# Attention scores kept in one PSUM bank per head: row maxima subtracted once per query block, later key tiles added as key differences

## The chip, the cores and the metric

One core of a Trainium2 chip runs the whole program. The metric is the device time of one execution in microseconds; the kernel before takes 2413.94 us (median of 3 runs, 2413.16 to 2414.01). Engines: TensorE (PE, its weight loads listed apart as PEld), VectorE (DVE), ScalarE (ACT), GpSimd (POOL) and SyncE (SP, which here only issues DMAs). Each engine works through its own queue strictly in the order in which the program was compiled.

## The reference

A transformer block with conditioning, on x of shape (2, 2048, 512) in float32:

```python
mod = silu(condition) @ Wada + bada            # shift, scale, gate, twice
xm = layernorm(x) * (1 + sc_a) + sh_a
q, k, v = split(xm @ Wqkv)                     # 16 heads of 32
scores = einsum('bhqd,bhkd->bhqk', q, k) * 32 ** -0.5
scores = where(causal, scores, -inf)
out = softmax(scores) @ v
x = x + gt_a * (out @ Wproj + bproj)
xm = layernorm(x) * (1 + sc_m) + sh_m
x = x + gt_m * (gelu(xm @ W1 + b1) @ W2 + b2)
```

What matters here is the softmax: the kernel computes exp(score - row maximum), so that every score tile needs the row maximum subtracted before the exponential.

## The kernel before

The two batch rows are done one after the other: QKV stage, attention phase, projection; then one MLP for both (W1 and W2 in a seven-product form whose weight sums are made on POOL ahead of time).

**QKV stage** (class `Qkv`, line 753). Tokens come in NG = 4 groups of 512. `group` (line 795) makes, for each of the C = 4 chunks f of 128 columns (four heads), q and then k as a transposed product of four accumulating matmuls (`ps_qk`, in a PSUM pool of 6 banks), and last four tiles of v. Of each q and k, ACT writes the high part (fp32r) and DVE the rest into a tile `hl` (a pool of 4 buffers), and SP stores it in DRAM (`qd`, `kd`). After chunk 0 of a group SP loads the keys and queries of that chunk back, with high and low parts stacked on the partitions: 4 heads x 32 become a contraction of 128 rows (kh, kl, kh, kl against qh, qh, ql, ql). Between the matmuls of groups 1 to 3 `among` puts **score banks** (`Row.score`, `bank`, lines 484 and 435): a 128-query by up to 512-key product on PE (tile `s`, 2 banks) whose maximum over the keys is taken by DVE. These only serve the row maxima.

**Quarters** (line 880) prepares the MLP weights: each `step` has POOL issue four DMAs of W1 or W2, wait for them, add and subtract five pairs, and issue the store. Sixteen steps are spread over the QKV stages, six in that of batch row 0 (group 3) and ten in that of row 1. Only instructions marked with `act` or `mm` keep the order in which they are written; the rest is put in order by the compiler's scheduler, so a quarter step may stand earlier in POOL's queue than its line suggests.

**Attention phase** (line 529). A unit is a pair (c, i) of a chunk of four heads and a block of 512 queries; there are 16 a row, in the order i = 0, 1, 2, 3 for c = 0 and 0, 2, 1, 3 after that. A unit has 4i + 3 steps, one key tile of 128 each (`steps_of`, line 646): 4i full tiles, then the diagonal ones: the whole-width tile, a step with the 384- and 128-wide tiles side by side, and the 256-wide one. `scores_t` (line 538) makes one step for the four heads:

- a matmul with `sel` (minus ones) and `fold[u % 2]` (rows of maxima, made by `rows` from one unit's maxima) starts a fresh bank `st` with the negative maximum of each query; four of them, one per head, each of 32 contraction rows;
- a matmul of the keys and queries adds the scores to that bank;
- ACT takes the exponential into a tile `e` (E_BUFS = 16, four steps' worth); on diagonal steps POOL masks it (`affine_select`, line 585);
- score banks of later units (up to AHEAD = 3 ahead) stand between these, as many as `due` and `count` ask for; within a step the third one borrows a bank of `st`.

Two steps later (LAG = 2) `flush` issues `values`, the product with v into `o`. Row sums go through POOL: `begin_chain` and `add_to` (lines 613 and 609) add the `e` of four steps and a product with ones (`sm`) follows; the last unit of a row adds on DVE. `finish` copies `o` and `sm` out.

Keys of the next chunk go to one of two tiles `kst0`, `kst1` in one load of 4 MB (line 672), used both by the score banks and by `scores_t`.

Of the kernel before, what the change touches and what calls it, by code (L numbers as in the profile page):

```python
# [8 lines left out]
F32 = mybir.dt.float32  # L9
# [18 lines left out]
def dit_block_kernel(  # L28
# [55 lines left out]
    def pool(name, bufs=1, **kw):  # L84
# [21 lines left out]
    tmask = bp.tile([P, TQ + 1], F32, tag="tmask", name="tmask")  # L106
    nc.vector.tensor_reduce(
        tmask[:, :TQ],
# [4 lines left out]
    nc.vector.tensor_copy(tmask[:, TQ:], tmask[:, TQ - 1 : TQ])  # L113
    fold, mhl = [], []
    for n in range(2):

        f = bp.tile([P, QB + P], F32R, tag=f"fold{n}", name=f"fold{n}")
        fold.append(f)
# [9 lines left out]
    def picks():  # L128
# [35 lines left out]
        [dram.tile([2, P, T], F32, tag=f"k{b}{c}", name=f"k{b}{c}") for c in range(C)]  # L164
        for b in range(B)
# [116 lines left out]
    class Row:  # L282


        def __init__(self, b):
            self.b = b
            self.vv = bp.tile([P, NT, D], F32, tag="vv", name="vv")
            self.kst, self.qst, self.pools = {}, {}, {0: bp}
# [12 lines left out]
        def load_keys(self, c, g, n=1):  # L301

            tok = slice(g * MT, (g + n) * MT)
            if g == 0:
                self.kst[c] = self.pools[c % 2].tile(
                    [P, HC, T], F32R, tag=f"kst{c % 2}", name="kst"
                )
            for r in range(4):
                nc.sync.dma_start(
                    self.kst[c][r * HD : (r + 1) * HD, :, tok].bitcast(F32),  # L310
                    kd[self.b][c][r % 2, :, tok].rearrange("(h d) t -> d h t", d=HD),
                )
# [122 lines left out]
        def bank(self, u, h, t, kb, s):  # L435
# [6 lines left out]
                self.kst[c][:, h, kb * QB : kb * QB + w],  # L442
# [41 lines left out]
        def score(self, n, borrow=None):  # L484

            for k in range(n):
                if borrow and k % 2 == 0:  # L490
                    s = borrow()
                else:
                    s = ps_sp.tile([P, QB], F32, tag="s", name="s")
                item = self.todo.pop(0)
                u = item[0]
                if self.mx is None:
                    self.mx = bp.tile(
                        [P, HC * TQ, units[u][1] + 1], F32, tag="mx", name="mx", bufs=3
                    )
                self.bank(*item, s)  # L500
                if not self.todo or self.todo[0][0] != u:
                    self.split(u, self.mx, s)
                    self.mx = None
                    self.at += 1

        def rows(self, u):
# [8 lines left out]
                fold[u % 2].rearrange("p (t q) -> p t q", t=TQ + 1),  # L515
                ps.unsqueeze(1).to_broadcast([P, TQ + 1, P]),
                tmask.unsqueeze(2).to_broadcast([P, TQ + 1, P]),
# [11 lines left out]
    def attention_phase(row):  # L529
        b, vv, kst, qst = row.b, row.vv, row.kst, row.qst  # L530
        with pool(f"att{b}") as ap, pool(
            f"ps_st{b}", bufs=HC, space=PSUM
        ) as ps_stp, pool(f"ps_o{b}", space=PSUM) as ps_op:
            row.pools[1] = ap

            n_bank = [0]

            def scores_t(u, step, n):
# [6 lines left out]

                def st_bank():

                    n_bank[0] += u == len(units) - 1  # L550
                    if n_bank[0] % 6 >= HC:
                        return ps_sp.tile([P, QB], F32, tag="s", name="st")
                    return ps_stp.tile([P, QB], F32, tag="st", name="st")

                c, i = units[u]
                tiles = steps_of[u][step]
                q0 = tiles[0][1]
                w = sum(QB - q for _, q in tiles)
                sts, es = [], []
                for h in range(HC):  # L560
                    g = slice(h * HD, (h + 1) * HD)
                    st = st_bank()
                    mm(
                        st[:, :w], sel[g, :], fold[u % 2][g, q0 : q0 + w],
                        start=True, stop=False,
                    )
                    sts.append(st)
                for h in range(HC):
                    at = 0
                    for j, q in tiles:  # L570
                        mm(
                            sts[h][:, at : at + QB - q],
                            kst[c][:, h, j * P : (j + 1) * P],
                            qst[u][:, h, q:],
                            start=False, stop=at + QB - q == w,
                        )
                        at += QB - q
                    e = ap.tile([P, QB], F32, tag="e", name="e", bufs=E_BUFS)
                    act(nc.scalar.activation(e[:, :w], sts[h][:, :w], AF.Exp))  # L579
                    if tiles[0][0] >= i * TQ:  # L580

                        d = e.rearrange("p (t k) -> p t k", k=P)[:, 0 : TQ : TQ - 1, :]
                        d = d[:, : len(tiles), :]
                        act(
                            nc.gpsimd.affine_select(  # L585
                                d, d, pattern=[[0, len(tiles)], [1, P]],
                                compare_op=ALU.is_ge, fill=0.0,
                                base=0, channel_multiplier=-1,
                            )
                        )  # L590
                    es.append(e)
                    if h < 2 and n >= 3 or h >= HC - n and n < 3:
                        row.score(1)
                if n >= 3:
                    row.score(1, st_bank)
                    row.score(min(n, HC) - 3)
                return es, max(0, n - HC)
# [42 lines left out]
            def flush(upto):  # L640
# [7 lines left out]
                + [[(i * TQ + 1, P), (i * TQ + 3, 3 * P)], [(i * TQ + 2, 2 * P)]]  # L648
# [882 lines left out]
```

## Time and profile before

| what | value |
|---|---|
| time, median of 3 runs | 2413.94 us |
| profiled execution, first to last instruction (span) | 2411.0 us |
| granted TensorE clock | 1.000 |
| st<-fold,sel matmuls | 1152, 148.6 us busy |
| POOL additions ee (row sums) | 592, 740.4 us busy |

The profiled execution has no separate timing; its span is 2.9 us below the median of the runs. Busy time of each engine by stage, in us, from the windows view:

| stage | from-to | us | PE | DVE | ACT | POOL | DMA share |
|---|---|---|---|---|---|---|---|
| QKV row 0, groups 0 (rest) to 3 | 40.0-212.8 | 172.8 | 172.8 | 91.8 | 31.9 | 41.4 | 0.66 |
| attention row 0 | 212.8-755.4 | 542.6 | 538.4 | 364.3 | 304.7 | 435.1 | 0.31 |
| projection row 0 | 755.4-812.1 | 56.7 | 56.7 | 38.0 | 4.3 | 32.1 | 0.76 |
| QKV row 1 | 812.1-1002.1 | 190.0 | 189.7 | 101.0 | 36.1 | 64.0 | 0.70 |
| attention row 1 | 1002.1-1543.7 | 541.6 | 537.7 | 364.1 | 304.6 | 435.0 | 0.31 |
| projection row 1, MLP | 1543.7-2411.0 | 867.3 | 856.5 | 368.3 | 204.4 | 111.4 | 0.34 |

A matmul's busy time runs from its start to its end, and the next one starts inside it, so PE is shown busy nearly everywhere; how dense it is must be read from the starts in the timeline. A line of the groups gives source line, engine, operation, output and input tiles, shapes, count, then busy time and mean duration, then idle time before and what ended it.

### The profile page before, as it was taken

The page shows a single profiled execution, that of the slowest core. Times are in us where ns is not written, and L with a number is a line of the kernel's source. Part 1 is how long each engine was busy: PE and PEld are TensorE (multiplying, and loading weights), DVE is VectorE, ACT ScalarE, POOL GpSimd, SP SyncE. Part 2 cuts the span into 40 slices and gives each one's busy share as a digit, 9 for nine tenths or more (in the row PEclk, how much of TensorE's full clock was granted, in tenths as well). Part 3 has the DMA queues.
Part 4 walks back from the last instruction along what each step waited for, and adds up shares of the span by engine and source line. Part 5 has one row for each costly group of instructions (what it writes and reads, how often), then busy time and mean ns, then how long its engine had stood idle before and what let it go on. Part 6 is the DMA issues. An engine that isn't in the chain of part 4 may idle for free.

```text
span 2411.0 us, 31023 instructions
## 1 busy us (share of the span) xinstructions
PE 2381.4 (99%) x10797; PEld 1167.1 (48%) x10797; DVE 1345.9 (56%) x2813; ACT 896.4 (37%) x1671; POOL 1125.3 (47%) x1279
## 2 busy tenths in 40 slices
PE   8999999999999999999999999999999999999998
PEld 4455555555544445555555554444444444444443
DVE  3466666766647446766676665663344263343424
ACT  2113555555563121355555555423213212312310
POOL 1062888978775560199897878432001101100200
PEclk9999999999999999999999999999999999999999
DMA  7677124051325794621505132552324233222323
GB/s 253 197 239 198 41 47 96 23 118 42 111 96 186 240 319 162 154 55 34 111 23 115 45 101 91 168 178 77 110 78 146 76 106 136 82 92 87 122 87 101
DMA packets 132854, 285.72 MB, mean 119 GB/s; under 512 B 13472, under 2 KB 42700, under 8 KB 127832
## 3 DMA queue, kind: packets, MB, share of 16 engines
q1 hardware_dynamic: 125936, 256.94, 36.1%
q0 software_dynamic: 6384, 26.25, 3.1%
q8 instruction: 85, 1.39, 0.2%
q14 instruction: 73, 0.60, 0.1%
q10 hardware_dynamic: 376, 0.55, 0.1%
HBM read 209.76 MB, written 81.79 MB: 121 GB/s over the span
## 4 chain that ended last, share of the span: by engine, by line
PE 96%; DVE 2%; POOL 1%; issue 0%; DMA 0%; ACT 0%; SPq 0%; DVEq 0%; POOLq 0%; ACTq 0%
PE st L199 19%; PE ps_h L199 16%; PE ps_y L199 16%; PE o L199 11%; PE s L199 10%; PE ps_qk L199 9%; PE ps_o L199 5%; PE ps_v L199 4%; PE sm L199 4%; PE ps_xt L207 1%; POOL ee L607 1%; PE ps_o L207 1%; DMA x<-in_x_dram 0%; DVE junk L449 0%; DVE mx L454 0%
## 5 line engine op out<-in xcount | busy, mean ns | idle before, releaser
L579 ACT ACTIVATE e<-st 128x512 f32<-128x512 f32 (+1 forms) x1152 | 574.7, 578 | 427.1 <-PE st L199 359.7
L607 POOL TENSOR_TENSOR ee<-ee,e 128x512 f32<-128x512 f32 x424 | 529.8, 1294 | 4.3 <-ACT e L579 4.0
L454 DVE TENSOR_REDUCE mx<-s 128x1 f32<-128x512 f32 x604 | 407.6, 687 | 203.6 <-PE s L199 202.5
L199 PE MATMUL s<-kst,qst 128*128 128x512 f32 (+3 forms) x1032 | 463.8, 451 | 4.7 <-DVE mx L454 2.9
L199 PE MATMUL st<-qst,kst 128*128 128x512 f32 (+3 forms) x1280 | 409.2, 387 | 0.0
L1295 POOL TENSOR_TENSOR c<-c 128x512 f32<-128x512 f32 x32 | 40.7, 1272 | 623.2 <-DVE c L1257 596.6
L199 PE MATMUL o<-e,vv 128*32 128x512 f32 (+3 forms) x2560 | 300.6, 538 | 2.0 <-POOL e L585 2.0
L199 PE MATMUL ps_h<-sx,w 128*128 128x512 f32 x640 | 286.7, 592 | 0.0
L449 DVE CUSTOM_DVE_ANT_0 junk<-s,causal 128x512 bf16<-128x512 f32 (+3 forms) x428 | 209.0, 488 | 132.9 <-PE s L199 125.2
L199 PE MATMUL ps_y<-sh,w 128*128 128x512 f32 x640 | 277.6, 592 | 0.0
L199 PEld LDWEIGHTS st<-qst,kst 128*128 128x128 f32 x1280 | 227.4, 188 | 94.2 <-issue 62.1
L199 PEld LDWEIGHTS s<-kst,qst 128*128 128x128 f32 x1032 | 194.4, 189 | 154.4 <-DVE mx L454 55.2
L607 POOL TENSOR_TENSOR ee<-e 128x512 f32<-128x512 f32 x168 | 210.6, 1288 | 100.8 <-ACT e L579 100.3
L199 PE MATMUL ps_qk<-xmT,wqkv 128*128 128x512 f32 x512 | 239.0, 594 | 1.8 <-DVE xmT L256 1.8
L1257 DVE TENSOR_TENSOR h<-c,ps_h 128x512 f32<-128x512 f32 x128 | 88.1, 688 | 232.4 <-PE ps_h L199 232.4
L585 POOL TENSOR_SCALAR_AFFINE_SELECT e<-e 128x128 f32<-128x128 f32 (+1 forms) x384 | 123.0, 364 | 195.7 <-ACT e L579 193.0
L199 PEld LDWEIGHTS ps_h<-sx,w 128*128 128x128 f32 x640 | 121.1, 190 | 150.2 <-issue 149.7
L199 PEld LDWEIGHTS ps_y<-sh,w 128*128 128x128 f32 x640 | 120.3, 190 | 144.9 <-issue 143.5
L1281 ACT ACTIVATE h<-h,cols 128x512 f32<-128x512 f32 x128 | 92.4, 722 | 182.0 <-DVE h L1257 182.0
L199 PE MATMUL st<-fold,sel 32*128 32x512 f32 (+1 forms) x1152 | 148.6, 481 | 0.6 <-ACT vv L836 0.2
L199 PEld LDWEIGHTS ps_qk<-xmT,wqkv 128*128 128x128 f32 x512 | 93.9, 190 | 96.9 <-issue 90.4
L199 PEld LDWEIGHTS st<-fold,sel 32*128 32x128 f32 x1152 | 59.1, 181 | 144.2 <-ACT e L579 86.6
(129 smaller groups left out, 2359.9 us busy)
## 6 DMA issues: line engine op xcount, KB each, us to landing
qst<-q SPq DMA_DIRECT2D x128, 256.0 KB
w<-w1d SPq DMA_DIRECT2D x34, 896.0 KB
w<-w2d SPq DMA_DIRECT2D x28, 1024.0 KB
kst<-k SPq DMA_DIRECT2D x24, 1024.0 KB
q<-hl SPq DMA_DIRECT2D x32, 512.0 KB
k<-hl SPq DMA_DIRECT2D x32, 512.0 KB
kst<-k SPq DMA_DIRECT2D x32, 256.0 KB
w<-in_L_cond_W_dram POOLq DMA_DIRECT2D x64, 128.0 KB, 5.6
```

Of the source, the lines that this page charges most:

```text
L199: return tc.keep_in_program_order(nc.tensor.matmul(*args, **kw))
L207: return tc.keep_in_program_order(nc.tensor.transpose(dst, src, ident[:n, :n]))
L449: nc.vector.tensor_tensor_reduce(junk[:, :w], s[:, :w], causal[:, QB - w :], 1.0, MASKED, ALU.add, ALU.max, m,)
L454: nc.vector.tensor_reduce(m, s[:, :w], axis=AX.X, op=ALU.max)
L579: act(nc.scalar.activation(e[:, :w], sts[h][:, :w], AF.Exp))
L585: nc.gpsimd.affine_select(d, d, pattern=[[0, len(tiles)], [1, P]], compare_op=ALU.is_ge, fill=0.0, base=0, channel_multiplier=-1,)
L607: act(engine.tensor_tensor(dst, x, y, ALU.add))
L1257: nc.vector.tensor_tensor(dst, x, y, op)
L1281: nc.scalar.activation(d, d, AF.Gelu, bias=col(r_b1 + chunk, 1))
L1295: nc.gpsimd.tensor_tensor(c1_, c1_, c2_, ALU.subtract)
```

## The change

A bank of scores now stays with its head for the whole unit. The first key tile adds the negative maxima and the scores as before; ACT reads the bank; the next tile adds the product of the queries with the **difference** of its keys and those of the tile before, in place, after the exponential has read the bank. So the `sel` matmul is issued once per head and unit instead of once per tile (unit 0 of each row keeps it, and the plain keys). The differences are made in the QKV stage by the new `gaps`, after each k: ACT copies the product into a tile `kf` whose first 128 columns POOL fills with the last tile of the previous group, DVE subtracts, ACT writes the high part, POOL the rest, and SP stores 512 KB in a new DRAM buffer `gd`.

With it: the pool of `hl` has 3 buffers, which q, k and the differences share; differences load into one tile `kgap` (16 DMAs of 256 KB per chunk, at the start of the phase and at three steps of a chunk's last unit and one of the next); the score banks keep a single tile of plain keys, reloaded head by head (`load_head`) after the last bank of each head; diagonal tiles pair up as (384), (256, 128), one after the other in the same bank, with `flush` between; score banks no longer borrow `st`; the last unit of a row no longer uses six banks.

```diff
-        f = bp.tile([P, QB + P], F32R, tag=f"fold{n}", name=f"fold{n}")
+        f = bp.tile([P, QB], F32R, tag=f"fold{n}", name=f"fold{n}")
...
+        def load_head(self, c, h):
+            for r in range(4):
+                nc.sync.dma_start(
+                    self.kst[r * HD : (r + 1) * HD, h, :].bitcast(F32),
+                    kd[self.b][c][r % 2, h * HD : (h + 1) * HD, :],
+                )
+        def load_gaps(self, c, g):
+            tok = slice(g * MT, (g + 1) * MT)
+            for r in range(4):
+                nc.sync.dma_start(
+                    self.kgap[r * HD : (r + 1) * HD, :, tok].bitcast(F32),
+                    gd[self.b][c][r % 2, :, tok].rearrange("(h d) t -> d h t", d=HD),
                 )
...
+                if i == NQ - 1 and c + 1 < C and self.todo[0][:2] != (u, h):
+                    self.load_head(c + 1, h)
...
-                for h in range(HC):
-                    g = slice(h * HD, (h + 1) * HD)
-                    st = st_bank()
-                    mm(
-                        st[:, :w], sel[g, :], fold[u % 2][g, q0 : q0 + w],
-                        start=True, stop=False,
-                    )
-                    sts.append(st)
-                for h in range(HC):
-                    at = 0
-                    for j, q in tiles:
+                keys = row.kgap if u else kst
...
+                for k, (j, q) in enumerate(tiles):
+                    if k:
+                        values()
+                    if j == 0 or u == 0:
+                        for h in range(HC):
+                            g = slice(h * HD, (h + 1) * HD)
+                            mm(
+                                sts[h][:, q:], sel[g, :], fold[u % 2][g, q:],
+                                start=True, stop=False,
+                            )
+                    for h in range(HC):
                         mm(
-                            sts[h][:, at : at + QB - q],
-                            kst[c][:, h, j * P : (j + 1) * P],
+                            sts[h][:, q:],
+                            keys[:, h, j * P : (j + 1) * P],
                             qst[u][:, h, q:],
-                            start=False, stop=at + QB - q == w,
+                            start=False, stop=True,
+                            skip_group_check=u > 0 and j > 0,
                         )
...
-                if n >= 3:
-                    row.score(1, st_bank)
-                    row.score(min(n, HC) - 3)
-                return es, max(0, n - HC)
+                return es, max(0, n - 3)
...
-                + [[(i * TQ + 1, P), (i * TQ + 3, 3 * P)], [(i * TQ + 2, 2 * P)]]
+                + [[(i * TQ + 1, P)], [(i * TQ + 2, 2 * P), (i * TQ + 3, 3 * P)]]
...
+        def gaps(self, g, f, ps, hp, tok):
+            kf = hp.tile([P, P + MT], F32, tag="kf", name="kf", bufs=2)
+            tail = self.tails[:, f, :]
+            if g == 0:
+                nc.gpsimd.memset(kf[:, :P], 0.0)
+            else:
+                nc.gpsimd.tensor_copy(kf[:, :P], tail)
+            nc.scalar.copy(kf[:, P:], ps)
+            if g + 1 < NG:
+                nc.gpsimd.tensor_copy(tail, kf[:, MT:])
+            d = kf[:, :MT]
+            nc.vector.tensor_tensor(d, kf[:, P:], d, ALU.subtract)
+            dl = hp.tile([P, 2, MT], F32R, tag="hl", name="dl", bufs=3)
+            nc.scalar.copy(dl[:, 0, :], d)
+            nc.gpsimd.tensor_tensor(dl[:, 1, :], d, dl[:, 0, :].bitcast(F32), ALU.subtract)
+            nc.sync.dma_start(
+                gd[self.row.b][f][:, :, tok].rearrange("l p t -> p l t"), dl.bitcast(F32)
             )
...
-                    hl = hp.tile([P, 2, MT], F32R, tag="hl", name="hl", bufs=4)
+                    hl = hp.tile([P, 2, MT], F32R, tag="hl", name="hl", bufs=3)
...
+                    if which == 1:
+                        self.gaps(g, f, ps, hp, tok)
```

## Prediction

> **What bounds the kernel now.** I read the page's busy shares first, then the costliest groups, then stretches of the attention phase, and last the timeline where the change acts. The page and two of its groups:
>
> ```profile
> PE 2381.4 (99%) x10797; PEld 1167.1 (48%) x10797; DVE 1345.9 (56%) x2813; ACT 896.4 (37%) x1671; POOL 1125.3 (47%) x1279
> ...
> L607 POOL TENSOR_TENSOR ee<-ee,e 128x512 f32<-128x512 f32 x424 | 529.8, 1294 | 4.3 <-ACT e L579 4.0
> ...
> L199 PE MATMUL st<-fold,sel 32*128 32x512 f32 (+1 forms) x1152 | 148.6, 481 | 0.6 <-ACT vv L836 0.2
> ```
>
> PE looks like the only bound, and the matmuls that the change removes are its own. But the shares are averages. Here are four units of chunk 1 of row 0 (i = 0, 2, 1, 3) and then the last unit, each from its first row-sum addition to that of the next; columns: length, then PE, PEld, DVE, ACT, POOL:
>
> ```profile
> 355.20:368.20 13.00, 13.00 (x125) 6.75 (x124) 5.95 (x12) 6.64 (x15) 2.81 (x9) 1.00 1.03 212
> 368.20:408.30 40.10, 40.10 (x255) 21.12 (x254) 29.12 (x62) 23.27 (x47) 38.30 (x41) 1.00 0.45 101
> 408.30:435.50 27.20, 26.87 (x191) 14.29 (x190) 19.02 (x62) 15.02 (x31) 23.43 (x29) 1.00 0.21 51
> 435.50:492.60 57.10, 57.10 (x373) 29.84 (x372) 39.59 (x99) 31.41 (x63) 54.32 (x56) 1.00 0.11 26
> ...
> 710.40:755.40 45.00, 44.46 (x330) 19.04 (x329) 33.58 (x51) 29.72 (x60) 12.94 (x17) 1.00 0.26 94
> ```
>
> POOL is busy 54.32 us of the 57.10 of an i = 3 unit: it stands just behind PE. At the end of such a unit the timeline shows PE already waiting for it:
>
> ```profile
> 542.29 2.52 POOL L585 TENSOR_SCALAR_AFFINE_SELECT e<-e 128x256 f32<-128x256 f32 x8
> ...
> 543.80 0.19 PEld L199 LDWEIGHTS o<-e,vv 128*32 128x32 f32 x8 [0.37 <-POOL e L585]
> ...
> 546.89 1.28 POOL L607 TENSOR_TENSOR ee<-e 128x512 f32<-128x512 f32 x1 [2.08 <-ACT e L579]
> ```
>
> So the loop is closed: POOL's masks release PE's value products, those release the next unit's scores, their exponentials release POOL's next additions.
>
> **Attention: what PE is spared.** Four `sel` matmuls and the next product in the timeline:
>
> ```profile
> 442.94 0.50 PE L199 MATMUL st<-fold,sel 32*128 32x512 f32 x4
> 443.38 0.50 PE L199 MATMUL st<-qst,kst 128*128 128x512 f32 x1
> ```
>
> The four hold PE for 443.38 - 442.94 = 0.44 us, 0.11 each. After the change a row issues 4 for each of 15 units and 16 in unit 0, 76, both rows 152; 1000 go, 110 us at PE's price. An i = 3 unit loses 14 of its 15 groups of four, 14 x 0.44 = 6.2 us.
>
> Weighed against this: the Trainium skill, "TensorEngine Tiling (Array Packing)", section "Theoretical Speedup", gives matmuls of at most 32 rows up to four times the speed. By it the four would cost about one 128-row slot (0.23 us, 444.06 to 444.30 in the same stretch), and I would estimate 57 us instead of 110. The trace shows 0.44, so the row decides.
>
> **Attention: what POOL lets through.** POOL's additions stay: 40 in an i = 3 unit, 28 in i = 2, 16 in i = 1. Back to back they take 1.25 us (eight in 10.0). Behind them stand the masks of the first two diagonal steps, now four 128-wide ones each, at 1.05 us for four. So POOL's chain from the first addition to the mask that releases PE is 40 x 1.25 + 2.1 = 52.1 us, and 37.1 and 22.1. From there to the next addition the trace shows 546.89 - 543.7 = 3.2 us here and 2.1 at the least elsewhere; without `sel` (0.44) and with a 384-wide tile alone, I take 2.5. Units can then not be shorter than 54.6, 39.6 and 24.6. PE alone would allow 57.1 - 6.2 = 50.9, so POOL decides. Savings of a row:
>
> - i = 3: 57.1, 57.1, 57.6 to 54.6: 8.0
> - i = 2: 42.4, 40.1, 40.4, 40.1 to 39.6: 4.6
> - i = 1: 25.4, 27.2, 26.7, 25.3 to 24.6: 6.2
> - i = 0: no additions on POOL, PE's price, 2 x 0.44 in three units: 2.7
> - the last unit adds on DVE (33.6 busy of 45): not POOL-bound; PE's price is 6.2, but it goes from six banks to four; I take 4
>
> Together 25.5, for two rows **-51**. Bounds: -110 if POOL did not bind, and about -20 if each of 32 units gave 1 us back. That upper end is for what before does not show: a bank's product now waits for the exponential of the same bank (ACT, four in 2.06 us), and the (256, 128) step does so twice, with four more exponentials a unit; and score banks take two PSUM banks and borrow none, so that a third score waits for DVE (0.69). Value products (1.0 us) and POOL's pace cover these in the units with i > 0; I take nothing. Queued behind such a wait on PE is everything, on ACT and POOL only work that depends on it.
>
> **Transfers.** Keys come twice (plain and differences): 256.94 MB at 36.1% of 2411 us is 0.295 MB/us, so 4 MB are 13.6 us of all 16 DMA engines. The attention phase uses 0.31 of them, so the sum fits. Chunk 0's differences must land before unit 1, and unit 0 is 17.5 us long. `load_head` waits for the last score bank of a head, and the next chunk's first bank is a step or two later; I take 3 us for six chunk changes, bounds 0 and 12.
>
> **QKV: what is added.** For each of 32 k tiles: ACT two copies (0.60 each in the `hl` rows), DVE one subtraction (0.69), POOL one subtraction (1.28, as in ee) and two 128-wide copies, SP one store (0.36 to issue). None of the engines is full: of 172.8 us DVE is busy 91.8, ACT 31.9, POOL 41.4. By throughput this is hidden, +0. But POOL's queue is in order, and the quarter steps stand in it:
>
> ```profile
> 127.09 4.32 POOL L923 DMA_DIRECT2D w<-in_L_cond_W_dram  x6 [108.69 <-DMA kst<-k]
> 135.53 0.73 POOL L931 TENSOR_TENSOR w<-w 128x256 f32<-128x256 f32 x1 [4.12 <-DMA w<-in_L_cond_W_dram]
> ...
> 149.22 1.46 POOL L923 DMA_DIRECT2D w<-in_L_cond_W_dram  x2 [3.88 <-DMA w1d<-w]
> ```
>
> This is the first of three pairs of steps, which run from 127.09 to 185.23 and mostly wait for their DMAs. In the compiled order of the changed program the POOL subtraction of group 2, chunk 2 stands behind the third pair. Its store is therefore late, and `hl` has three buffers shared by q, k and differences, so the difference of chunk 3 gets its buffer only when that store has landed. SP holds at that store, with the q and k stores and x loads behind it. ACT waits for the buffer at its high copy; behind it on ACT stand the next `hl` copies and v; behind those on DVE `hl`'s low part and then score maxima; PE goes on through its six product banks (four v, q, k of the next group) until its third score finds both score banks taken. Before, that score is here (group 3):
>
> ```profile
> 172.60 0.79 PE L199 MATMUL s<-kst,qst 128*128 128x512 f32 x1
> ```
>
> Steps end at 185.2, plus 2 for a later start and 4 for the additions now among them: 191. Subtraction 1.3, store 4 to land (a store of keys and its reload take 5.5), two ACT copies, `hl` and a maximum on DVE 2.6: PE goes on at about 199, +26. An earlier hold of some 10 us behind the first pair is contained in this, since the steps set the time. In row 1 the subtraction of group 0, chunk 2 stands in the fourth pair, just ahead of this store:
>
> ```profile
> 880.84 0.55 POOL L911 DMA_DIRECT2D w2d<-w  x1
> ```
>
> 880.8 + 4 + 1.3 is 886.1; with 4 and 2.6 as above PE goes on at 892.7. Before, the same third score starts at 865.94: +27. For the two-bank running afterwards I add 2 to each: **+57**. Bounds: +35 (stores landing at once, steps 8 us earlier each) and +75 (stores land later, since the DMA share is 0.96 in the first half of row 1's stage, and its later pairs hold again).
>
> **Sum.** 2411.0 - 51 + 3 + 57 = 2420; the median stands 2.9 us above the span, so **2423**. About 0.2% (4.8 us) is what a measurement can tell from no change.
>
> **Rivals.**
> - *The waits in QKV are covered.* POOL has 131 us idle in that stage, so the steps might end before PE needs the banks. This one ends on the other side: 2414 - 51 + 3 = 2366 with nothing lost. It decides below a QKV loss of 48 us. Against it: the order in POOL's queue is fixed, and 58 us of steps cannot hide behind six banks (about 20 us of products).
> - *POOL does not bind.* The additions' 3.2 us gap closes and PE's price counts: 2414 - 110 + 3 + 57 = 2364. Against it: 54.32 of 57.10 busy and the wait at 543.80.
> - *The attention gain is eaten* by the in-place waits on exponentials and the two score banks, 1 us a unit: 2414 - 20 + 3 + 57 = 2454.
> - That `sel` would not go is excluded by the compiled order: 152 are left.
>
> **How the numbers follow.** Forecast .55 (own range 2405 to 2440), QKV covered .17 (2350 to 2390), POOL not binding .08, gain eaten .20 (2440 to 2465). The range 2370 to 2458 leaves out half of the second, nearly all of the third, and little of the last: .18. Faster by over 0.2% (under 2409): .17 + .08 + .07 of the forecast's own = .32. Within: .13. Slower: .35 + .20 = .55.
>
> **What the changed profile would show.** st<-fold,sel x152. Stages of QKV at about 201 and 219 us instead of 172.8 and 190.0, with PE idle in one block each, an ACT wait at the difference's high copy for a DMA out of its buffer, and the POOL subtraction right behind a quarter step. Units of i = 3 at 54.6 with POOL back to back at 1.25 and more of PE's waits put down to POOL's masks. I am wrong in the attention part if such units are at 51 (POOL does not bind) or at 57 (banks), in the QKV part if the stages stay within 10 us of before.

## Result and profile after

The changed kernel takes 2513.7 us (median of 4 runs, 2512.0 to 2515.6) against 2414.0: slower by a ratio of 1.0414, 95% interval 1.0399 to 1.0428. The profiled execution's span is 2513.9 us. Forecast were 2423 and a range up to 2458.

The page after, with the lines that answer to those of before, and the two lines of the score banks, whose products are written to the tile `s`:

```profile
PE 2362.2 (94%) x9797; PEld 1114.6 (44%) x9797; DVE 1378.2 (55%) x2844; ACT 971.0 (39%) x1863; POOL 1185.0 (47%) x1367
...
L202 PE MATMUL s<-kst,qst 128*128 128x512 f32 (+3 forms) x1280 | 590.6, 473 | 109.9 <-DVE mx L472 53.5
...
L617 POOL TENSOR_TENSOR ee<-ee,e 128x512 f32<-128x512 f32 x424 | 528.9, 1291 | 8.5 <-ACT e L587 8.1
...
L202 PEld LDWEIGHTS s<-kst,qst 128*128 128x128 f32 x1280 | 236.4, 190 | 463.3 <-DVE mx L472 240.8
```

The additions on POOL are what they were (1.29 us each), and 1000 matmuls are gone (152 with `sel` are left). But PE, 99% busy before, is at 94%, and it now stands before the score banks (`s`), waiting for DVE's maxima (`mx`). The page before has for these products 4.7 us of idle time instead of 109.9:

```profile
L199 PE MATMUL s<-kst,qst 128*128 128x512 f32 (+3 forms) x1032 | 463.8, 451 | 4.7 <-DVE mx L454 2.9
```

Of the 109.9 us, 44.7 are two long holds in the QKV stages (19.97 and 24.76 us, shown below); the rest is in shorter waits. The 1280 products are no new work: all of them are now called `s`, where before 248 used a bank of `st`.

By stage (windows view after; columns as before: length, PE, PEld, DVE, ACT, POOL, granted clock, DMA share, GB/s):

```profile
40.00:248.80 208.80, 179.94 (x518) 88.19 (x516) 101.81 (x237) 48.70 (x86) 64.39 (x95) 0.93 0.65 210
248.80:804.30 555.50, 520.08 (x3167) 248.75 (x3166) 368.48 (x865) 324.00 (x673) 438.59 (x494) 1.00 0.44 110
861.90:1086.80 224.90, 193.98 (x534) 94.47 (x532) 113.96 (x251) 54.68 (x98) 90.13 (x145) 0.95 0.69 226
1086.80:1646.50 559.70, 524.68 (x3166) 251.26 (x3166) 367.83 (x860) 323.18 (x671) 438.09 (x494) 0.99 0.43 109
```

| stage | before | forecast | after |
|---|---|---|---|
| QKV row 0 | 172.8 | 201 | 208.8 (+36.0) |
| attention row 0 | 542.6 | 519 | 555.5 (+12.9) |
| QKV row 1 | 190.0 | 219 | 224.9 (+34.9) |
| attention row 1 | 541.6 | 518 | 559.7 (+18.1) |

(Forecast of attention: half of -51 + 3 for each row.) QKV lost 71 us where 57 were forecast. Attention was to gain 48 and lost 31: of the 91 us between forecast and measurement, 79 are there. In row 0's attention phase PE does less (520.1 us busy instead of 538.4) in a longer time, so it waits.

### The profile page after: what moved, and what is told of

Same layout as the page of the kernel before. It is cut to its first block, busy times and chain, and to the rows that moved or that the text cites. A ratio compares the mean times of both kernels' runs of the same rounds, so it can differ in the third digit from the quotient of the medians.

```text
span 2513.9 us, 29463 instructions
## 1 busy us (share of the span) xinstructions
PE 2362.2 (94%) x9797; PEld 1114.6 (44%) x9797; DVE 1378.2 (55%) x2844; ACT 971.0 (39%) x1863; POOL 1185.0 (47%) x1367
## 4 chain that ended last, share of the span: by engine, by line
PE 82%; DVE 8%; DMA 5%; POOL 3%; issue 1%; ACT 1%; SPq 0%; DVEq 0%; POOLq 0%; ACTq 0%
PE ps_h L202 15%; PE ps_y L202 15%; PE s L202 13%; PE o L202 10%; PE st L202 9%; PE ps_qk L202 6%; PE ps_o L202 4%; DVE mx L472 4%; PE sm L202 4%; PE ps_v L202 3%; DMA w<-in_L_cond_W_dram 2%; DVE junk L467 2%; POOL w L971 1%; PE ps_xt L210 1%; DMA k<-hl 1%
## 5 line engine op out<-in xcount | busy, mean ns | idle before, releaser
L587 ACT ACTIVATE e<-st 128x512 f32<-128x512 f32 (+3 forms) x1280 | 610.4, 535 | 418.1 <-PE st L202 367.7
L202 PE MATMUL s<-kst,qst 128*128 128x512 f32 (+3 forms) x1280 | 590.6, 473 | 109.9 <-DVE mx L472 53.5
L472 DVE TENSOR_REDUCE mx<-s 128x1 f32<-128x512 f32 x768 | 518.2, 689 | 208.7 <-PE s L202 201.9
L202 PEld LDWEIGHTS s<-kst,qst 128*128 128x128 f32 x1280 | 236.4, 190 | 463.3 <-DVE mx L472 240.8
L202 PE MATMUL st<-qst,kgap 128*128 128x512 f32 (+3 forms) x1248 | 392.7, 376 | 0.0
L467 DVE CUSTOM_DVE_ANT_0 junk<-s,causal 128x128 bf16<-128x128 f32 (+3 forms) x512 | 249.0, 486 | 155.7 <-PE s L202 146.1
L202 PEld LDWEIGHTS st<-qst,kgap 128*128 128x128 f32 x1248 | 221.8, 189 | 77.3 <-ACT e L587 40.4
L596 POOL TENSOR_SCALAR_AFFINE_SELECT e<-e 128x128 f32<-128x128 f32 (+1 forms) x384 | 128.8, 374 | 116.6 <-ACT e L587 114.7
L202 PE MATMUL ps_v<-wqkv,xmT 128*128 128x512 f32 x256 | 122.8, 596 | 2.8 <-ACT xmT L264 2.8
L1394 ACT ACTIVATE yt<-yt,gbias,gb 128x512 f32<-128x512 f32 (+1 forms) x33 | 26.3, 800 | 253.6 <-DVE yt L1297 253.6
```

Of the source, the lines that this page charges most:

```text
L202: return tc.keep_in_program_order(nc.tensor.matmul(*args, **kw))
L467: nc.vector.tensor_tensor_reduce(junk[:, :w], s[:, :w], causal[:, QB - w :], 1.0, MASKED, ALU.add, ALU.max, m,)
L472: nc.vector.tensor_reduce(m, s[:, :w], axis=AX.X, op=ALU.max)
L587: nc.scalar.activation(es[h][:, at : at + QB - q], sts[h][:, q:], AF.Exp)
L596: nc.gpsimd.affine_select(d, d, pattern=[[0, len(tiles)], [1, P]], compare_op=ALU.is_ge, fill=0.0, base=0, channel_multiplier=-1,)
L1394: nc.scalar.activation(yt[chunk][g][:, tok], yt[chunk][g][:, tok], AF.Identity, bias=gbias[:, chunk, b : b + 1], scale=gb[:, chunk, b : b ...
```

## Experiments

Two theories stood against each other for the attention phase. **P**: POOL's additions pace the units, as the prediction has it, so PE's saving shows only in part. **B**: the score banks, on two PSUM banks that no longer borrow from `st`, make PE wait for DVE in every step. Names beginning with b_ are made from the kernel before, with a_ from the changed one. Differences of b_ runs from "before" are taken from the kernel before as measured beside them (2413.5 to 2415.1 us), those of a_ runs from the changed kernel's 2513.7.

### The parts of the change, one by one

**b_nosel**, the saving alone:

```diff
-                    mm(
-                        st[:, :w], sel[g, :], fold[u % 2][g, q0 : q0 + w],
-                        start=True, stop=False,
-                    )
+                    if step == 0 or u == 0:
+                        mm(
+                            st[:, :w], sel[g, :], fold[u % 2][g, q0 : q0 + w],
+                            start=True, stop=False,
+                        )
...
-                            start=False, stop=at + QB - q == w,
+                            start=at == 0 and step > 0 and u > 0, stop=at + QB - q == w,
```

> The kernel before, with the sel matmul only on the first step of a unit (and all of unit 0); the later products start their bank afresh, so the maximum is not subtracted there (left out). Everything else, six banks included, as before. If POOL's additions pace the units, as predicted: 2414 - 51 = about 2360. If PE alone does: 2414 - 110 = about 2304.

2378.9 us, 35.0 less than before. Far from PE's price, so something else paces; but also less than 51, so neither number expected is met.

**b_two_banks**, the score banks of the change alone (without a third bank, a fourth score of a step, where there is one, also moves behind that step, as in the changed kernel):

```diff
-                    row.score(1, st_bank)
-                    row.score(min(n, HC) - 3)
-                return es, max(0, n - HC)
+                    row.score(1)
+                return es, max(0, n - 3)
...
-                    if n_bank[0] % 6 >= HC:
-                        return ps_sp.tile([P, QB], F32, tag="s", name="st")
```

> The kernel before with the score banks on their two PSUM banks alone: no bank of st is borrowed, and the last unit keeps to four banks, as in the changed kernel. Sel matmuls stay. If two banks are covered (the prediction, nothing taken): 2414 to 2420. If PE's waits for DVE at the score banks are what ate the attention gain (82 us between predicted and measured): 2460 to 2500.

2488.2 us, **+74.4**. No `sel` is removed, no difference made, no bank held: this one edit costs three quarters of what the whole change costs (99.7). The last units of the rows, which lose their six banks, are 2.3 us longer each; the rest is spread over the other units (the i = 3 unit of chunk 1, from one copy of `o` to the next: 57.4 to 61.4). One line of the waits before and the same of b_two_banks (waiting engine and tile, for what: us in total, times, longest):

```profile
PEld s L199 <- DVE mx L454: 55.2, 80, 0.8
```
```profile
PEld s L199 <- DVE mx L454: 140.4, 282, 1.1
```

What is to be seen is the number of times: 80 waits become 282, none longer than 1.1 us. No single place stands out, which is why neither a page of totals nor the chain of the kernel before warns of it.

**b_two_nosel**, both edits:

> The kernel before with both: score banks on two PSUM banks and no later sel matmuls (the maximum is not subtracted there). Two banks cost 74.4 us, sel gave 35.0. If the two add: 2453. If the saved PE time is used up by the same waits at the score banks: 2470 to 2488. The changed kernel without its QKV work is at 2441; the distance to it is what keeping the bank and the new diagonal steps do.

2434.7 us: `sel` gives more here (53.5) than with borrowed banks (35.0). Neither of the two numbers expected: the parts don't add, two banks cost 55.8 with `sel` gone and 74.4 with it.

**a_nogaps**, the changed kernel without its QKV work:

```diff
                     if which == 1:
-                        self.gaps(g, f, ps, hp, tok)
+                        pass
...
-                    gd[self.b][c][r % 2, :, tok].rearrange("(h d) t -> d h t", d=HD),
+                    kd[self.b][c][1, :, tok].rearrange("(h d) t -> d h t", d=HD),
```

with `bufs=4` for `hl`. The true differences are left out.

> The changed kernel without the work on differences in the QKV stage, hl with four buffers again; the differences are loaded from the low parts of the keys instead (left out: the true differences), with the same DMAs. If the QKV stages' loss is that work: they return to 173 and 190 us, 2514 - 71 = about 2443, and the attention phase stays at 555 to 560 us a row. If later stages carry part of it, less.

2441.3 us. The QKV stages are at 173.8 and 189.4 us, and the attention phase stays at 556.5 and 555.4. The two halves of the loss are independent, but for some 4 us: row 1's attention phase takes 559.7 in the changed kernel, with the QKV work ahead of it.

These runs give the account, each step the difference of two measured kernels (in another order the steps would have other sizes, since the parts don't add):

| from | to | us |
|---|---|---|
| before (2413.8 beside this run) | without later sel (b_nosel, 2378.9) | -35.0 |
| | score banks on two banks (b_two_nosel, 2434.7) | +55.8 |
| | held banks, new diagonal steps, loads (a_nogaps, 2441.3) | +6.6 |
| | differences in the QKV stage (after, 2513.7) | +72.4 |

### What the two banks cost, and why

The chain of waits in an i = 2 unit of the changed kernel (start, us, what) repeats every 3.4 us:

```profile
566.85 0.45 PE s L202
...
567.32 0.70 DVE mx L472
...
568.07 0.50 PE s L202
568.57 0.46 PE st L202 x2
...
569.21 1.00 PE o L202 x8
570.20 0.45 PE s L202
...
570.67 0.70 DVE mx L472
...
571.42 0.50 PE s L202
```

and the load of the weights for the score product at 568.07, from the timeline:

```profile
568.07 0.19 PEld L202 LDWEIGHTS s<-kst,qst 128*128 128x128 f32 x1 [0.53 <-DVE mx L472]
```

The score product at 566.85 fills one bank and DVE takes its maximum (0.70). The next score goes to the other bank meanwhile; the one at 568.07 needs the first bank again and starts only when DVE has read it. So with two banks taking turns DVE's reading lies in PE's chain once a step, and PE stands for part of it. The value products (`o`, at 569.21), which the prediction set against such a wait, come behind these scores in PE's order and cannot fill it. In the kernel before PE had a third bank in hand there, and the chain of an i = 3 unit (435 to 493 us) ran through PE alone.

**a_half_max** shortens DVE's reading and leaves the banks:

```diff
-                nc.vector.tensor_reduce(m, s[:, :w], axis=AX.X, op=ALU.max)
+                nc.vector.tensor_reduce(m, s[:, : w // 2], axis=AX.X, op=ALU.max)
```

> The changed kernel with the maxima of full score banks taken over the first 256 of 512 keys (left out: the other half), so that DVE reads a bank in about 0.4 instead of 0.69 us; matmuls and banks are unchanged. If PE waits at the two banks for DVE's reading: attention shortens by 15 to 30 us a row, 2455 to 2485. If the number of banks costs through something else (PE's order, POOL): 2505 to 2514.

2467.9 us, 45.8 less than after; attention 533.1 and 536.7 instead of 555.5 and 559.7, and the i = 3 units come to 54.1 to 55.3 us, as long as those of b_nosel. So it is DVE's reading that PE waits for. The same cut was not run on the kernel before, so 45.8 is not the price of the banks; that is b_two_banks's.

**a_halfadd** and **b_nosel_halfadd** cut POOL's additions, in the changed kernel and in the kernel before without `sel`:

```diff
-                for h in range(HC):
+                for h in range(2 if u < len(units) - 1 else HC):
                     add(u, h, chain[h], chain[h], es[h])
```

> The changed kernel with only two of four heads added on POOL in add_to, but for each row's last unit (left out: part of the row sums). The same cut gave 46 us where six banks serve the scores and sel is gone. If POOL's additions pace the changed kernel as well: 2460 to 2475. If the score banks pace it and POOL only follows: 2500 to 2514.

> The kernel before without the later sel matmuls (2378.9 us), and in add_to only two of four heads are added on POOL, but for each row's last unit (left out: part of the row sums). If POOL's additions are why 35 us came instead of PE's 110: with 26 instead of 40 additions in an i = 3 unit POOL no longer paces, and most of the missing 75 us come, 2305 to 2330. If something else (the score banks, DVE) holds PE there: 2365 to 2380.

2507.4 and 2332.5 us: the same cut gives 46.3 us where six banks serve the scores (a little less than expected), and 6.3 in the changed kernel. There the i = 3 units stay as they are (56.8, 59.0, 57.8 us, against 56.9, 59.0, 57.7); nearly all of the 6.3 comes from the i = 1 unit ahead of each row's last (23.2 to 20.0). An i = 3 unit (row 0, chunk 2, from one copy of `o` to the next) of the kernel before, of b_nosel, of b_nosel_halfadd and of after:

```profile
576.80:634.50 57.70, 57.29 (x380) 29.85 (x372) 39.13 (x99) 31.47 (x63) 52.78 (x58) 1.00 0.10 24
```
```profile
566.80:621.50 54.70, 52.31 (x324) 26.86 (x316) 39.09 (x99) 31.94 (x63) 52.53 (x58) 1.00 0.10 25
```
```profile
552.80:605.10 52.30, 51.13 (x324) 26.46 (x316) 39.05 (x99) 31.93 (x62) 35.75 (x44) 1.00 0.11 26
```
```profile
627.80:685.50 57.70, 54.30 (x318) 25.60 (x313) 38.86 (x97) 33.10 (x66) 52.08 (x58) 1.00 0.39 89
```

In the second, POOL (the fifth busy time) fills 52.5 of 54.7 us, and the unit is as long as the prediction's bound (54.6). Take 14 of its 40 additions away and PE, 51.1 us busy, sets 52.3. In the fourth POOL is as busy, but 5.6 us of the unit are free of it and PE is 3.4 us short of full: nothing is full, PE and DVE wait for each other. Theory P holds where there are enough banks; in the changed kernel B does, and P is hardly felt.

**a_spread** was to place the same score banks further apart:

```diff
+                    if h == 1 and slots[0]:
+                        slots[0] -= 1
+                        row.score(1)
```

in the loop of value and sum products, that is between heads 1 and 2, and after heads 0 and 2 of the scores.

> The changed kernel with the same score banks, but placed apart: after heads 0 and 2, then between the second and third head of the value or sum products, instead of after heads 0, 1, 3 and one behind the other. If the loss by two banks (74 us in the kernel before) is that scores stand too close for DVE's 0.69 us each: attention shortens by 15 to 40 us a row, 2435 to 2485. If two banks cost the same wherever the scores stand: 2505 to 2520.

2738.9 us, 225 worse, far outside both expectations, and for a reason of its own, so it says nothing on the banks. Its chain of waits:

```profile
565.57 0.98 PE o L202 x4
566.55 0.43 PE s L202
566.98 0.98 PE o L202 x4
```

Four value products (two heads) take 0.98 us; all eight took 1.00 when they stood together. By these times the heads' products, which lie in different 32 columns of PE, run side by side, and a full-width product between them makes two rounds out of one. The Trainium skill, "TensorEngine Tiling (Array Packing)", section "Key Properties", says that a change of tiling mode drains the engine. The row agrees that the halves no longer overlap.

**a_add_dve** takes four additions a unit from POOL to DVE (the last argument):

```diff
                     elif i and n_step == i * TQ:
-                        add_to(u, chain, es)
+                        add_to(u, chain, es, True)
```

> The changed kernel with the additions of the first diagonal step on DVE instead of POOL: four of 40 in an i = 3 unit, 0.73 instead of 1.25 us each. If POOL's chain still sets the unit's length: some 3 us in each of 22 units, about 2450. If DVE, with its score maxima, is now what PE waits for: 2514 to 2540.

2609.8 us, 96 worse, the way that theory B expects but beyond its range. In the chain of waits four additions on POOL (5.00 us from 698.99) and a mask stand ahead of the four on DVE (2.92 us from 704.27), and the next maxima behind these; DVE's own waits for those exponentials and masks are at most 12 us in all. The mean granted clock is also lower (0.965, after 0.987), so part of the 96 us is likely to be clock. How much belongs to which is not separated; the run supports B but does not measure it.

### The QKV stage

The hold that the prediction describes is in the trace. Three lines of POOL's and one of ACT's timeline after, in row 0 (the last store of the quarter steps, the tail copy, the late subtraction; then ACT's high copy), and PE's third score product in row 0 and in row 1:

```profile
196.29 0.59 POOL L951 DMA_DIRECT2D w1d<-w  x1 [0.30 <-POOL w L971]
196.88 0.30 POOL L823 COPY tails<-kf 128x128 f32<-128x128 f32 x1
197.13 1.26 POOL L828 TENSOR_TENSOR dl<-kf,dl 128x512 fp32r<-128x512 f32 x1
...
201.74 0.62 ACT L827 CAST dl<-kf 128x512 fp32r<-128x512 f32 x1 [20.14 <-DMA g<-dl]
...
206.40 0.80 PE L202 MATMUL s<-kst,qst 128*128 128x512 f32 x1 [19.97 <-DVE mx L472]
...
941.38 0.69 PE L202 MATMUL s<-kst,qst 128*128 128x384 f32 x1 [24.76 <-DVE mx L467]
```

ACT waits 20.14 us for a buffer of differences to be stored. Meanwhile PE stands for 19.97 us, until the third score product at 206.4; in row 1 it stands for 24.76. The chain of waits over row 0's stage names what the steps themselves waited for:

```profile
142.65 8.89 DMA w<-in_L_cond_W_dram
...
154.23 7.16 DMA w1d<-w
```

On POOL the two show as 6.24 and 5.50 us of idle time, where the same steps before wait 4.12 at most. The steps end at 196.9 instead of 185.8.

**a_off_pool**:

```diff
-            nc.gpsimd.tensor_tensor(dl[:, 1, :], d, dl[:, 0, :].bitcast(F32), ALU.subtract)
+            nc.vector.tensor_tensor(dl[:, 1, :], d, dl[:, 0, :].bitcast(F32), ALU.subtract)
```

and so for the memset and both tail copies.

> The changed kernel with the tail copies and the low part of the differences on DVE instead of POOL; three shared buffers stay. If the wait comes from the places behind the quarter steps in POOL's queue: most of the 71 us go, about 2450. If it comes from three buffers and the stores' landing themselves, or DVE's queue becomes the bound: 2490 to 2514.

2478.0 us: 35.8 of the 72.4 go; the stages are 190.5 and 203.0. The 20 us hold is gone, but that is half of the loss, not "most" of it.

**a_four**, in addition, without `kf` (ACT copies the tails, DVE makes the low part) and with four buffers:

```diff
+            dl = hp.tile([P, 2, MT], F32R, tag="hl", name="dl", bufs=4)
+            d = dl[:, 1, :].bitcast(F32)
+            p = dl[:, 0, :].bitcast(F32)
...
+                nc.scalar.copy(p[:, :P], tail)
+            nc.scalar.copy(p[:, P:], ps[:, : MT - P])
+            nc.vector.tensor_tensor(d, ps, p, ALU.subtract)
```

> The changed kernel with the differences made without the tile kf (the shifted product is put in dl itself by ACT, the tail copies by ACT, the low part by DVE), and in the room this gives hl has four buffers. Off POOL alone gave 2478 us, with stages of 190.5 and 203.0 us. If the rest of the QKV loss (some 31 us in both rows) is the wait for one of three buffers: 2445 to 2455. If it is ACT and DVE handing to each other in order: 2470 to 2480.

2465.1 us, another 12.8, all in row 1: its stage (196.0) and the first unit behind it, which is 5.6 us shorter. It lies between the two expectations.

**b_hl3**, the kernel before with three buffers of `hl`:

> The kernel before with three hl buffers instead of four, nothing else. If three buffers are too few by themselves: 2425 to 2440. If they only hurt with a third user whose store comes late: 2412 to 2418.

2420.6 us, +7.2 (ratio 1.0033, 1.0022 to 1.0043): also between. Three buffers cost a little by themselves, and more when a third user holds one.

So of 72.4 us, 35.8 come from work in POOL's queue among the quarter steps, 12.8 from the buffers, `kf` and the tail copies' engine together, and 23.8 remain in a_four (2465.1 against 2441.3). For these there is only the trace of a_off_pool: in row 0 PE stands 6.5 us at the transposes for group 3, while DVE is busy 19.5 of the 21 us from 126 to 147 and a store of keys takes 6.4 us to land. No run separates the two; this part stays open.

### A version that keeps the banks free

`sel` is worth its 35 us only if it goes without taking banks. **b_rows** puts the maximum into the contraction instead, in place of the product of the two low parts, which it leaves out:

```diff
-                    kd[self.b][c][r % 2, :, tok].rearrange("(h d) t -> d h t", d=HD),
+                    neg[:, tok].unsqueeze(1).to_broadcast([HD, HC, n * MT])
+                    if r == 3
+                    else kd[self.b][c][r % 2, :, tok].rearrange("(h d) t -> d h t", d=HD),
...
+            for h in range(HC):
+                nc.sync.dma_start(
+                    self.qst[u][3 * HD :, h, :].bitcast(F32),
+                    fold[u % 2][h * HD : (h + 1) * HD, :QB].bitcast(F32),
+                )
...
-                            kst[c][:, h, j * P : (j + 1) * P],
-                            qst[u][:, h, q:],
-                            start=False, stop=at + QB - q == w,
+                            kst[c][:rows, h, j * P : (j + 1) * P],
+                            qst[u][:rows, h, q:],
+                            start=step > 0, stop=True,
```

where `rows` is 96 on a unit's first step (which keeps `sel`) and 128 after it, and `neg` is a DRAM buffer of -1.

> The kernel before, where the maximum is subtracted by the product itself after the first step of a unit: the fourth 32 rows of the contraction (low part of the keys against low part of the queries, left out) hold -1 for the keys and the unit's rows of maxima for the queries, copied there by four DMAs a unit; score banks contract over the first 96 rows. No bank is held and no difference is made. If the loss of the change lies in held banks and QKV work alone, the 35 us of the run without sel come: 2370 to 2385. If the DMAs of the maxima come late for the second step: 2400 to 2440.

2437.1 us. Most units are as short as in b_nosel, but the ends of u0, u4 and u8 (units counted within a row) are 9 to 11 us late: PE waits for the copied maxima.

**b_rows_sums** and **b_sums** take the first diagonal step's additions off POOL, with and without that edit:

```diff
-                        if k == TQ - 1 and n_step + 1 < i * TQ:
+                        if k == TQ - 1:
                             sums_of, wait = (chain, False), 2
-                    elif i and n_step == i * TQ:
-                        add_to(u, chain, es)
-                        sums_of, wait = (chain, False), 2
```

> As b_rows, and the first diagonal step of a unit goes to the row sums by a product with ones on PE (1.0 us) instead of four additions on POOL (5.0 us). If POOL's additions pace the units once sel is gone and six banks serve the scores: i = 3 units come to some 52 us, 2335 to 2360. If PE paces them: 24 us more than b_rows.

> The kernel before with that row-sum edit alone; sel stays. PE paces these units: 22 products of 1.0 us more, up to 2436. If POOL paced the kernel before: faster, 2380 to 2405.

2421.8 us, 15.4 less than b_rows, which neither expectation has; and 2425.9 us, 11.0 more than before. The i = 3 units go from 54.7 to 55.3 us down to 52.6 to 54.4 in the first, and from 56.5 to 57.6 up to 56.8 to 58.4 in the second. The same edit gains where POOL paces and loses where PE does: in the kernel before, PE set the pace, with POOL just behind it. Only half of the 22 us that the products cost on PE come through there, so POOL held some of it too.

**b_rows_i0** and **b_rows_sums_i0** keep `sel` in the i = 0 units, to take the wait away:

```diff
+                whole = step > 0 and i > 0
+                rows = P if whole else 3 * HD
```

> As b_rows, but units with i = 0 keep sel for all three steps and copy no maxima. In b_rows the three such units of a row that stand beside a 4 MB load of keys (u0, u4, u8) are 28.6 us a row longer than without sel, with PE waiting for the copy of the maxima. If that wait is the whole distance between 2437 and 2379: 2375 to 2388. If the copies also come late elsewhere: 2400 to 2430.

> As b_rows_i0, with the first diagonal step summed on PE instead of POOL. b_rows_sums stood 15 us below b_rows, mostly in units with i = 3 (53.4 to 54.7). If POOL paces those units: 2355 to 2372, below the other by as much again. If not: equal to it or above.

2435.5 and 2426.0 us: no gain to speak of, both outside what was expected. The place of the wait was taken one unit too early: a unit's copy of `o`, by which its end was read, comes two steps into the next unit, so the late ones were the second steps of u1, u5 and u9. The waits of b_rows_sums_i0:

```profile
PE st L204 <- DMA qst<-fold: 52.2, 6, 10.0
```

**b_rows_late_keys** takes b_rows_sums_i0 and issues the next chunk's keys later, with SP's order for these DMAs written out:

```diff
-                if u % NQ == 0 and c + 1 < C:
-                    row.load_keys(c + 1, 0, NG)
...
+                    if u % NQ == 1 and n_step == 2 and c + 1 < C:
                         row.load_keys(c + 1, 0, NG)
```

> As b_rows_sums_i0, and the 4 MB load of the next chunk's keys is issued in the second unit of a chunk, behind the copies of the maxima in SP's queue, instead of at the start of the first. The runs with i = 0 units on sel did not lose the wait: it moved to the next unit's second step, still 52 us in six places for a copy of 256 KB. If that copy waits behind the keys' load: these 52 us go, 2365 to 2380, below the kernel before. If the copies are late by themselves: 2415 to 2430.

**2358.6 us**, 0.9767 of the kernel before (0.9754 to 0.978), and 67 us less than b_rows_sums_i0, where 52 were waits for the copy; that is somewhat better than expected. No wait for `qst<-fold` is left among PE's. A copy of 256 KB had been standing behind a load of 4 MB: in b_rows_sums_i0 the load for chunk 2 of row 0 is issued at 353.64 and the copy for u5 at 363.92, and PE goes on at 380.50; here the copies at 356.02 and 368.33 are issued ahead of the load at 370.81. The mean granted clock of the attention phases also rises, from 0.97 to 1.00, which goes with the other 15 us, but no run separates it. The attention phase of row 0 and the same i = 3 unit as above:

```profile
216.10:729.60 513.50, 498.35 (x3282) 254.96 (x3282) 358.71 (x856) 308.11 (x607) 381.02 (x448) 1.00 0.32 84
564.50:618.50 54.00, 52.88 (x336) 27.18 (x328) 39.09 (x99) 32.01 (x62) 48.62 (x55) 1.00 0.14 40
```

In this unit POOL has 5.4 us to spare again, and PE is full but for 1.1.

## Why the prediction was wrong

- **The step that failed** is the sentence on the score banks in "what POOL lets through": two banks and no borrowing, "Value products (1.0 us) and POOL's pace cover these in the units with i > 0; I take nothing". The two banks cost 74.4 us in the kernel before and 55.8 with `sel` gone. The value products don't cover the wait, since in PE's order they come behind the scores that wait for one another; and POOL's pace does not, since the units grow past POOL's bound (57.7 us with POOL 52.1 busy). DVE, at 39.6 of 57.1 us, looked far from full, but a wait for DVE needs no full DVE: PE stops at each 0.7 us reading whose bank it needs next. The rival "the attention gain is eaten" was this, with the right name but about half the price: 1 us a unit against 55.8 / 32 = 1.7 to 74.4 / 32 = 2.3. The prediction's own sign of it also came: i = 3 units "at 57 (banks)", here 56.9 to 59.0. With the other parts the attention phases come to -35.0 + 55.8 + 6.6 = +27.4 us where the prediction has -51 + 3 = -48.
- **PE's price for `sel`** (110 us) is reached by no run; the nearest is b_nosel_halfadd with 81.8 us (against its own 2414.4), where half of one kind of addition is gone too. What those additions alone are worth in the kernel before was not run, so 81.8 is not all `sel`'s; the row that the prediction went by, 0.44 us for four products, still stands for 110. The four times of the Trainium skill, "TensorEngine Tiling (Array Packing)", section "Theoretical Speedup", which the page calls an upper end, would have allowed an estimated 57 in all. In this case's rows four products of 32 rows take 0.44 us against 4 x 0.23 for full ones, about twice the speed.
- **POOL as the bound** was the right mechanism for the saving taken alone: 54.1, 55.3 and 54.7 us for i = 3 units against 54.6 reckoned. The size was off: -35.0 instead of -51. From one copy of `o` to the next, row 0 gains 7.4 us in the i = 3 units (8.0 reckoned) and 4.5 in those with i = 2 (4.6), but only 1.4 with i = 1 (6.2), 1.2 with i = 0 (2.7) and 1.8 in the last one (4): the miss is in the short units, which came to 25.4 to 26.6 us with i = 1 instead of 24.6, and in the last. What holds them there stays open.
- **Held banks, the new diagonal steps and the loads per head**: 3 us taken, 6.6 measured together.
- **QKV**: the mechanism is shown, in the places named (ACT's wait for a DMA out of the difference's buffer, the subtraction right behind a quarter step, the third score product). The term was 57 and measured 72.4. In row 0 the prediction let the steps end at 191 and PE go on at 199; they ended at 196.9 and PE went on at 206.4, with longer waits of the steps for their own DMAs. That the new stores lengthen these is likely, but no run shows it. The earlier hold (6.9 us, before the transposes for group 3) is contained in this, as said. In row 1 PE goes on 25.6 us later in the stage than before, close to the 27 forecast; some 9 us come in smaller pieces, where 2 were taken. The one long hold thus explains most of row 1's loss, and the forecast's shortfall is spread over both rows.
- That a difference adds no throughput problem was right; that this makes it free was not claimed, and the rival that the waits are covered is out, at a QKV loss of 72.4 where it needed less than 48.

## What to carry to other kernels

Before an edit that pins a buffer, ask who borrowed it: the price is paid by the borrower, in many short waits, and a run with the buffers alone finds it. Measure the gain of a removed instruction by leaving it out first: here it was 35 us as long as another engine's work stayed where it was. When a wait stays after an edit that should have removed it, look for the place where it stands now before changing more: here it belonged to the next unit.

## What the runs showed of the hardware

- After standing still, PE got a lower granted clock (windows of the changed kernel, PE's busy time second, clock third from the end):

```profile
190.00:200.00 10.00, 0.00 (x0) 0.00 (x0) 0.00 (x0) 0.00 (x0) 8.47 (x14) 0.56 0.52 207
200.00:210.00 10.00, 3.60 (x6) 1.86 (x7) 4.52 (x9) 3.61 (x6) 3.11 (x4) 0.50 0.89 318
210.00:220.00 10.00, 10.00 (x28) 5.28 (x27) 6.42 (x15) 1.80 (x3) 1.56 (x2) 0.92 1.00 242
```

  In finer windows it is 1.00 up to 190 us (PE stands from 186.4), 0.50 from 192 to 211, and 1.00 again from 212, where PE had gone on at 206.4. From this we estimate that the hold of 20 us costs some 2.5 us more than itself (about 5 us at half the clock). The two QKV stages with holds have a mean of 0.93 and 0.95, those of the kernel before 1.00.
- Value products of two heads take as long as those of four (0.98 and 1.00 us): side by side by columns, two more cost nearly nothing. Four `sel` products, side by side by rows, take 0.44 us, about two slots of a full one.
- POOL's waits for its own DMAs in row 0's QKV stage grew (4.12 at most to 6.24 us) when SP's stores were added. The mean DMA share of the stage did not rise (0.66 before, 0.65 after), but from 140 to 160 us, where the two longest waits are, it was 0.94 and 1.02 in the two halves, against 0.49 and 0.69 before.
